# Giving the chain between two scans priority in an interleaved Mamba, FFN and attention kernel

## The chip, the cores and the metric

The kernel runs on one core of one Trainium2 chip. The time is that of the whole program on the device, in microseconds (us), and the figure compared is the median of several runs. Before the change it is 2910.93 us, the median of 3 runs that lie between 2910.67 and 2912.76 us.

A core has five engines, each with a queue of its own that runs in a fixed order: TensorE (PE, matrix products and transposes; its weight loads appear as PEld), VectorE (DVE), ScalarE (ACT), GpSimd (POOL) and SyncE (SP, which here only issues transfers). An instruction waits at the head of its queue until the semaphores it needs are set, and all that stands behind it on that engine waits too.

## The reference, cut to what matters

The input x holds 16 images of 512 positions and 256 channels in float32. Four blocks are added to it in turn:

```python
x = x + mamba(layernorm(x))
x = x + ffn(layernorm(x))
x = x + linear_attention(layernorm(x))
x = x + ffn(layernorm(x))
```

The Mamba block is a recurrence over the 512 positions, with 16 states for each of the 256 channels:

```python
x_in = x @ w_in
dt_low, B, C = split(x_in @ w_x)
dt = softplus(dt_low @ w_dt + b_dt) * 0.099 + 0.001
inp_term[n] = sum_d(dt[d] * A[d, n] * B[n] * x_in[d])      # A = -exp(A_log)
h = exp(dt * A) * h + inp_term
y = h @ C + Dp * x_in
```

The input term has no channel index: it is summed over the channels, so one set of 16 sequences feeds the recurrences of all channels. The feed-forward network (FFN) quantises its input in blocks of 16 to a four-bit grid and back, forms silu(gate) * up with 704 columns, quantises that too, and multiplies by w_down. The attention has 16 heads of 16 channels with the feature map elu + 1 and causal running sums.

## The kernel before, in words

**One image at a time through the scans, the others around it.** The scans of an image are 16 steps in `mamba` (L445). In each, DVE runs one scan instruction over a 128x1024 tile (L485: 128 pairs of channel and state, two such groups one behind the other) and one multiply by C (L489). The tile `bar` of decay factors for it is made by ACT: two exponentials (L466) of a tile `sp` that a transfer has brought (L454: dt, written to DRAM before and read back so that each channel's row lies on 16 partitions), then a square (L469). There are two buffers for `bar` and three for `sp`. PE sums each pair of steps over the states into `py` (L495), which was begun with Dp times u (L483); after eight steps ACT copies `py` to `yT` (L500). Two such copies make y of an image; it is turned by eight transposes into two banks `pt_y` (L508) and DVE adds these to x (L511). x is kept as four chunks of 128 positions.

**What comes before the scans.** `front` (L382) normalises the next image (`layernorm`, L349) and turns it into features (`to_features`, L370); its copies are made while the image before is scanned. `prologue` (L389) then makes, from these features, in this order: z, as `pz` (PE, L396; the product of w_in, w_x and w_dt is folded into one matrix before the loop), with Abs (L405) and Relu (L406) on ACT; u (L412); softplus by Tanh and Ln on ACT (L414, L415) and one multiply-add on DVE (L416), which gives dt; eight transfers of dt to DRAM on SP's queue (L421); C's copy `cm` (L426); dt times u on DVE (L430); its product with A, `pg` (PE, L433); B as `pbm` (PE, L396 again); a copy of it into the tile `inp` (ACT, L439); the multiply of the copy with `pg` (DVE, L440); a copy of that result over the first half of the tile (ACT, L441). The first scan needs `inp`.

The tiles of this chain are shared: `soft`, `dtu` and `yT` are one buffer in turn, and so are `dt` and `inp`; u and cm have one buffer each. z's Abs of the next image therefore can't write before yT of this image has been read by its transposes. PSUM has seven banks in common use (tag "bank": pz, pg, pbm, pt, po and so on, in turn) and one for `py`.

**The FFN.** `ffn` (L517) is called with names that end in `_f` for the first FFN and `_g` for the second: layernorm (bn_stats, the variance plus epsilon at L359, its power -1/2 on POOL at L361 as `rstd`, the normalised chunks at L364 as `xn`), then `fp4` (L208 to L236: on DVE block maxima `amax` at L212, their scales from L217 on, `v` at L226; on ACT `big` at L230; on DVE L232 twice and L234, which writes the quantised values back into the tile), then `tT` (the transposes `pt` at L376, the copies at L377). Then for each of the four chunks and each half of the 704 columns: `pg`, `pu` (PE, L535), Tanh `sg` (ACT, L541), L542 and L545 (DVE); `fp4` again on the chunk's hidden layer; transposes `pt_h` (L561) and copies `hqT` (L565, L570); the product `po` (L574) and its addition to x (L578).

**The interleaving.** All these are Python generators that yield pieces of cost. While image b is scanned, the last FFN of image b-2 runs among its scans; then the first FFN of b and the attention of b-1 take turns, and the pieces of `prologue` for image b+1 are dealt out among the pieces of the first FFN of b (`first`, L781, `weave`, L772, `by_turns`, L811). So the end of the scans of image b, its y, the begin of its first FFN, and the chain from z to the input term of image b+1 stand close together in the program, from the last scan of b to the first scan of b+1: this stretch is called the turn below. Before the loop, `prologue(0)` and `mamba(0)` are woven with the quantisation of the FFN weights (`ffn_weights`, names ending in `_wg`, `_wu`, `_wd`).

**What sets the order.** The framework (Tile) orders the instructions itself before the program runs: among those that are ready in its own model of the machine, it issues the one with the lowest priority number, and an instruction's number is its place in the program text as the generators lay it out. The orders that come out are fixed in each engine's queue.

Of the kernel before, what the change touches and what calls it, by code (L numbers as in the profile page):

```python
# [10 lines left out]
F32 = mybir.dt.float32  # L11
BF16 = mybir.dt.bfloat16
AF = mybir.ActivationFunctionType
ALU = mybir.AluOpType
# [3 lines left out]
P = 128  # L18
# [14 lines left out]
def kernel(  # L33
# [18 lines left out]
    nc = tc.nc  # L52
    B, S, D = x.shape
# [5 lines left out]
    NC = S // P  # L59
    ND = D // P  # L60
# [8 lines left out]
    DT_MIN, DT_MAX = 0.001, 0.1  # L69
# [319 lines left out]
    def prologue(b):  # L389

        xnT = turned.pop(b)

        def from_xn(w, name):
            p = bank(f"{name}_{b}")
            for k in range(ND):
                nc.tensor.matmul(p, w[:, k], xnT[:, k, :], start=(k == 0), stop=(k == ND - 1))  # L396
            return p

        soft = one.tile([P, ND, S], F32, tag="soft", name=f"soft_{b}")
        dt = one.tile([P, ND, S], F32, tag="dt", name=f"dt_{b}")
        for e in range(ND):
            pz = from_xn(w_z_sb[:, :, ts(e, P)], f"pz{e}")
            nc.scalar.activation(soft[:, e, :], pz, AF.Abs, bias=b_dt_sb[:, e : e + 1])  # L405
            nc.scalar.activation(  # L406
                dt[:, e, :], pz, AF.Relu, bias=b_relu[:, e : e + 1], scale=DT_MAX - DT_MIN
            )
        yield 0.5
        u = one.tile([P, ND, S], F32, tag="u", name=f"u_{b}")  # L410
        for e in range(ND):
            nc.scalar.copy(u[:, e, :], from_xn(w_in_sb[:, :, ts(e, P)], f"pu{e}"))  # L412
        yield 0.5
        nc.scalar.activation(soft, soft, AF.Tanh, scale=0.5)  # L414
        nc.scalar.activation(soft, soft, AF.Ln, bias=half_c, scale=0.5 * LN_C)  # L415
        nc.vector.scalar_tensor_tensor(dt, soft, DT_MIN - DT_MAX, dt, ALU.mult, ALU.add)  # L416

        dd = dram.tile([ND, 2, 32, 2, S], F32, tag="dt", name=f"dd_{b}")
        for e in range(ND):
            for q in range(4):  # L420
                nc.sync.dma_start(  # L421
                    dd[e, q // 2, :, q % 2, :], dt[32 * q : 32 * q + 32, e, :]
                )
        yield 1.5
        cm = one.tile([P, S], F32, tag="cm", name=f"cm_{b}")
        nc.scalar.copy(cm, from_xn(w_c_sb, "pcm"))  # L426


        dtu = one.tile([P, ND, S], F32, tag="soft", name=f"dtu_{b}")
        nc.vector.tensor_tensor(dtu, dt, u, ALU.mult)  # L430
        pg = bank(f"pg_{b}")
        for k in range(ND):
            nc.tensor.matmul(  # L433
                pg, a_rep[:, k].rearrange("p n i -> p (n i)"), dtu[:, k, :],
                start=(k == 0), stop=(k == ND - 1),
            )
        pb = from_xn(w_b_sb, "pbm")
        inp = one.tile([P, 2, S], F32, tag="dt", name=f"inp_{b}")
        nc.scalar.copy(inp[:, 0, :], pb)  # L439
        nc.vector.tensor_tensor(inp[:, 1, :], inp[:, 0, :], pg, ALU.mult)  # L440
        nc.scalar.copy(inp[:, 0, :], inp[:, 1, :])  # L441
        begun[b] = (u, dd, inp, cm)
        yield 2.5

    def mamba(b, xt):  # L445
        u, dd, inp, cm = begun.pop(b)

        yT = one.tile([P, ND, S], F32, tag="soft", name=f"yT_{b}")

        def spread(e, j, q0):  # L450

            sp = one.tile([P, 2, S], F32, tag="sp", name=f"sp_{b}_{e}_{j}_{q0}", bufs=NSP)
            src = dd[e, q0 // 2, j * G8 : (j + 1) * G8].rearrange("i q t -> i (q t)")
            nc.sync.dma_start(  # L454
                sp.rearrange("p q t -> p (q t)"),
                src.unsqueeze(0).to_broadcast([NS, G8, 2 * S]),
            )
            return sp

        def decay(sp, e, j, q0):  # L460

            bar = bars[state["bar"] % NBAR]
            state["bar"] += 1
            for i in range(2):
                g = 16 * e + 4 * (q0 + i) + j
                nc.scalar.activation(  # L466
                    bar[:, i, 1:S], sp[:, i, 1:S], AF.Exp, scale=a_col[:, g : g + 1]
                )
            nc.scalar.activation(bar[:, :, 1:S], bar[:, :, 1:S], AF.Square)  # L469
            return bar  # L470

        steps = [(e, j, q0) for e in range(ND) for j in range(4) for q0 in (0, 2)]
        sps = [spread(*steps[at]) for at in range(NSP - 1)]
        ahead = decay(sps[0], *steps[0])
        for at, (e, j, q0) in enumerate(steps):
            bar = ahead
            if at + NSP - 1 < len(steps):
# [7 lines left out]
            nc.vector.tensor_tensor_scan(  # L485
                h.rearrange("p i t -> p (i t)"), bar.rearrange("p i t -> p (i t)"),
                inp.rearrange("p i t -> p (i t)"), 0.0, ALU.mult, ALU.add,
            )
# [12 lines left out]
            yield 3.5  # L501


        for c in range(0, NC, 2):
            pt = bank(f"pt_y_{b}_{c}")
            for i in range(2):
                for e in range(ND):
                    nc.tensor.transpose(  # L508
                        pt[:, ts(i * ND + e, P)], yT[:, e, ts(c + i, P)], ident
                    )  # L510
            nc.vector.tensor_tensor(  # L511
                xt[:, c : c + 2, :], xt[:, c : c + 2, :],
                pt.rearrange("p (c d) -> p c d", d=D), ALU.add,
            )
        yield 1.5

    def ffn(i, nm, xt):  # L517
# [358 lines left out]
```

## Time and profile before

| what | value |
|---|---|
| median of 3 runs | 2910.93 us |
| the profiled execution | 2910.69 us, of which the span of the trace is 2908.9 us |
| mean granted TensorE clock in it | 0.915 |
| scans L485, 256 of them | 578.1 us busy on DVE, 2277 ns each |
| multiplies L489, 256 | 309.2 us busy on DVE, 1213 ns each |
| squares L469, 256, and exponentials L466, 512 | 269.8 and 348.7 us busy on ACT |
| share of the chain that ended last | DVE 55%, PE 29%, ACT 7% |
| POOL busy | 4% |

The span is the time from the first to the last instruction that the profile has; the time of the execution holds 1.8 us more around it. [...] In the view of the groups, each line gives line number, engine, operation, output and inputs by the program's names, busy time in us, and the idle time of the engine just before these instructions with what ended it. In the timeline, a row's first two numbers are start and length in us from the span's start, and square brackets hold the idle time before it and what ended that. In the table of windows, each row is one stretch of time: its bounds and length, then the busy us of PE, PEld, DVE, ACT and POOL in this order (with the number of instructions in parentheses), then the mean granted clock of TensorE, then the transfers' share and rate.

### The profile page before, as it was taken

The numbers are of one execution on the slowest core, as the hardware profiler recorded it, in microseconds if no ns is written. First come the engines' busy times: TensorE is split into PE (matmuls) and PEld (weight loads), VectorE is DVE, ScalarE is ACT, GpSimd is POOL, SyncE is SP. The second block draws the span as 40 slices with busy tenths as digits, with TensorE's granted clock in tenths as the row PEclk, the third lists the DMA queues.
The fourth block names the chain that finished last, engine by engine and source line by source line (L and its number), as shares of the span: only waits on it lengthen the run. The fifth ranks groups of instructions, "written<-read, shape, count | busy, mean of one in ns | idle before, by whom it ended". The sixth has DMA issues, their size and how long they took to land.

```text
span 2908.9 us, 33292 instructions
## 1 busy us (share of the span) xinstructions
PE 2441.2 (84%) x12639; PEld 1428.2 (49%) x12639; DVE 2545.1 (87%) x3795; ACT 1349.0 (46%) x2286; POOL 121.1 (4%) x153
## 2 busy tenths in 40 slices
PE   5676888888888988888888888888888888887887
PEld 2233545454554545455454545545455454545555
DVE  7897889989899898989989898998989999898565
ACT  5555454454545445453545445444544544542122
POOL 2000000000000000000000000000000000000000
PEclk8787899998998999899999999999999899989898
DMA  5332112031321313122031321303122130310000
GB/s 159 87 80 73 51 44 80 15 95 44 80 59 29 81 29 86 53 61 63 21 88 44 80 58 44 80 15 95 44 80 59 36 81 22 84 47 8 1 1 15
DMA packets 64372, 165.21 MB, mean 57 GB/s; under 512 B 8434, under 2 KB 26836, under 8 KB 64212
## 3 DMA queue, kind: packets, MB, share of 16 engines
q1 hardware_dynamic: 62592, 162.03, 21.4%
q8 instruction: 99, 1.62, 0.2%
q10 hardware_dynamic: 1620, 1.06, 0.1%
q14 instruction: 61, 0.50, 0.1%
HBM read 146.28 MB, written 16.78 MB: 56 GB/s over the span
## 4 chain that ended last, share of the span: by engine, by line
DVE 55%; PE 29%; ACT 7%; issue 5%; POOL 2%; POOLq 0%; DVEq 0%; ACTq 0%
DVE h L485 16%; DVE h L489 7%; PE pqk L607 3%; DVE sm L660 2%; PE po_g L574 2%; PE pg_f L535 2%; PE pu_f L535 2%; PE pg_g L535 2%; DVE amax_f L212 2%; PE pu_g L535 2%; PE pz L396 2%; PE py L495 2%; DVE h_f L234 1%; DVE v_f L232 1%; DVE v_f L226 1%
## 5 line engine op out<-in xcount | busy, mean ns | idle before, releaser
L485 DVE TENSOR_TENSOR_SCAN h<-bar,inp 128x1024 f32<-128x1024 f32 x256 | 578.1, 2277 | 10.1 <-ACT inp L441 8.9
L466 ACT ACTIVATE bar<-sp,a_col 128x511 f32<-128x511 f32 x512 | 348.7, 715 | 411.3 <-DVE h L485 410.8
L495 PE MATMUL py<-h,red 128*32 128x512 f32 x1024 | 271.4, 684 | 89.1 <-DVE h L489 89.1
L489 DVE TENSOR_TENSOR h<-h,cm 128x1024 f32<-128x1024 f32 x256 | 309.2, 1213 | 0.0
L469 ACT ACTIVATE bar<-bar 128x1022 f32<-128x1022 f32 x256 | 269.8, 1054 | 4.5
L574 PE MATMUL po_g<-wdT,hqT_g 128*128 128x256 f32 (+1 forms) x768 | 199.8, 403 | 33.1 <-ACT hqT_g L565 33.1
L574 PE MATMUL po_f<-wdT,hqT_f 128*128 128x256 f32 (+1 forms) x768 | 204.7, 410 | 7.8 <-ACT hqT_f L565 7.7
L535 PE MATMUL pg_f<-wgT,tT_f 128*128 128x352 f32 x512 | 200.5, 517 | 2.5 <-DVE sm L660 2.2
L535 PE MATMUL pu_f<-wuT,tT_f 128*128 128x352 f32 x512 | 180.0, 475 | 14.4 <-DVE sm L660 14.4
L574 PEld LDWEIGHTS po_f<-wdT,hqT_f 128*128 128x128 f32 (+1 forms) x768 | 141.4, 197 | 96.3 <-issue 26.8
L574 PEld LDWEIGHTS po_g<-wdT,hqT_g 128*128 128x128 f32 (+1 forms) x768 | 138.3, 193 | 94.3 <-ACT hqT_g L565 47.2
L535 PE MATMUL pg_g<-wgT,tT_g 128*128 128x352 f32 x512 | 178.4, 471 | 0.0
L535 PE MATMUL pu_g<-wuT,tT_g 128*128 128x352 f32 x512 | 173.5, 461 | 0.0
L660 DVE TENSOR_TENSOR sm<-psc,causal 128x512 f32<-128x512 f32 x256 | 163.5, 680 | 9.9 <-PE psc L653 7.9
L230 ACT ACTIVATE big_f<-v_f 128x704 bf16<-128x704 f32 (+1 forms) x80 | 67.3, 841 | 203.2 <-DVE v_f L226 203.0
L535 PEld LDWEIGHTS pu_f<-wuT,tT_f 128*128 128x128 f32 x512 | 100.9, 199 | 79.1 <-DVE sm L660 21.7
L607 PE MATMUL pqk<-tT_a,w_qkv_sb 128*128 128x512 f32 x256 | 135.6, 670 | 0.7 <-ACT tT_a L377 0.7
L535 PEld LDWEIGHTS pg_g<-wgT,tT_g 128*128 128x128 f32 x512 | 97.8, 195 | 74.9 <-issue 37.1
L535 PEld LDWEIGHTS pg_f<-wgT,tT_f 128*128 128x128 f32 x512 | 94.7, 205 | 70.5 <-issue 17.7
L535 PEld LDWEIGHTS pu_g<-wuT,tT_g 128*128 128x128 f32 x512 | 98.1, 192 | 55.1 <-issue 1.5
L495 PEld LDWEIGHTS py<-h,red 128*32 128x32 f32 x1024 | 36.4, 114 | 176.8 <-DVE h L489 118.0
L541 ACT ACTIVATE sg_g<-pg_g 128x352 f32<-128x352 f32 x128 | 58.8, 459 | 108.2 <-PE pg_g L535 108.0
(224 smaller groups left out, 4483.8 us busy)
## 6 DMA issues: line engine op xcount, KB each, us to landing
sp<-dd SPq DMA_DIRECT2D x256, 512.0 KB, 4.6
x<-in_L_attn_a_x_dram SPq DMA_DIRECT2D x16, 512.0 KB, 4.7
dd<-dt SPq DMA_DIRECT2D x128, 64.0 KB, 1.7
out_dram<-x SPq DMA_DIRECT2D x16, 512.0 KB, 3.0
w_qkv_sb<-in_L_attn_b_W_attn_dram ACTq DMA_DIRECT2D x1, 768.0 KB, 6.8
raw_d<-in_L_ffn_w_down_dram SPq DMA_DIRECT2D x1, 704.0 KB
raw_g<-in_L_ffn_w_gate_dram SPq DMA_DIRECT2D x1, 640.0 KB, 6.4
raw_u<-in_L_ffn_w_up_dram SPq DMA_DIRECT2D x1, 640.0 KB, 6.2
```

What stands on the lines that cost most here:

```text
L212: nc.vector.tensor_reduce(amax, src.rearrange("p (b k) -> p b k", k=BLK), AX.X, ALU.max, apply_absolute_value=True,)
L230: nc.scalar.activation(big, v, AF.Abs, scale=STEP)
L466: nc.scalar.activation(bar[:, i, 1:S], sp[:, i, 1:S], AF.Exp, scale=a_col[:, g : g + 1])
L469: nc.scalar.activation(bar[:, :, 1:S], bar[:, :, 1:S], AF.Square)
L485: nc.vector.tensor_tensor_scan(h.rearrange("p i t -> p (i t)"), bar.rearrange("p i t -> p (i t)"), inp.rearrange("p i t -> p (i t)"), 0.0, ...
L489: nc.vector.tensor_tensor(h, h, cm.unsqueeze(1).to_broadcast([P, 2, S]), ALU.mult)
L495: nc.tensor.matmul(py[32 * q : 32 * q + 32, :], red[:, j, :], (h0, h)[q // 2][:, q % 2, :], start=False, stop=(j == 3),)
L535: nc.tensor.matmul(pw[:, :HF], xqT[:, k, ts(c, P)], wT[:, k, cols], start=(k == 0), stop=(k == ND - 1),)
L541: nc.scalar.activation(sg, pg[:, :HF], AF.Tanh, scale=0.5)
L574: nc.tensor.matmul(po[:, :D], hqT[:rows, r, :], wdT[:rows, r, :], start=(r == 0), stop=(r == NR - 1),)
L607: nc.tensor.matmul(pz, w_qkv_sb[:, k, ts(je, P)], xnT[:, k, :], start=(k == 0), stop=(k == ND - 1),)
L660: nc.vector.tensor_tensor(t, psc[g].rearrange("p (s t) -> p s t", t=P), causal.unsqueeze(1).to_broadcast([P, NH // 4, P]), ALU.mult,)
```

## The change

Five blocks of the program text are wrapped in `with tc.high_priority():`. Instructions that are issued inside it get the priority numbers of the program's begin instead of that of their place, so that in the framework's ordering they go ahead of all other instructions that are ready at the same time. What they wait for stays the same. The blocks are, in `prologue`: z with its Abs and Relu; u; Tanh, Ln, dt and the transfers of dt; C's copy, dt times u, `pg`, `pbm` and the three instructions on `inp`. In `mamba`: the copy `yT`, and the turning of y with its addition to x. The rest of the program, the sizes, the buffers and the number of instructions are as before. The lines move: what is L485 before is L489 after, L489 is L493, L416 is L419, L440 is L444, L535 is L541.

```diff
@@ -396,50 +396,54 @@
                 nc.tensor.matmul(p, w[:, k], xnT[:, k, :], start=(k == 0), stop=(k == ND - 1))
             return p
 
-        soft = one.tile([P, ND, S], F32, tag="soft", name=f"soft_{b}")
-        dt = one.tile([P, ND, S], F32, tag="dt", name=f"dt_{b}")
-        for e in range(ND):
-            pz = from_xn(w_z_sb[:, :, ts(e, P)], f"pz{e}")
-            nc.scalar.activation(soft[:, e, :], pz, AF.Abs, bias=b_dt_sb[:, e : e + 1])
-            nc.scalar.activation(
-                dt[:, e, :], pz, AF.Relu, bias=b_relu[:, e : e + 1], scale=DT_MAX - DT_MIN
-            )
+        with tc.high_priority():
+            soft = one.tile([P, ND, S], F32, tag="soft", name=f"soft_{b}")
+            dt = one.tile([P, ND, S], F32, tag="dt", name=f"dt_{b}")
+            for e in range(ND):
+                pz = from_xn(w_z_sb[:, :, ts(e, P)], f"pz{e}")
+                nc.scalar.activation(soft[:, e, :], pz, AF.Abs, bias=b_dt_sb[:, e : e + 1])
+                nc.scalar.activation(
+                    dt[:, e, :], pz, AF.Relu, bias=b_relu[:, e : e + 1], scale=DT_MAX - DT_MIN
+                )
         yield 0.5
-        u = one.tile([P, ND, S], F32, tag="u", name=f"u_{b}")
-        for e in range(ND):
-            nc.scalar.copy(u[:, e, :], from_xn(w_in_sb[:, :, ts(e, P)], f"pu{e}"))
+        with tc.high_priority():
+            u = one.tile([P, ND, S], F32, tag="u", name=f"u_{b}")
+            for e in range(ND):
+                nc.scalar.copy(u[:, e, :], from_xn(w_in_sb[:, :, ts(e, P)], f"pu{e}"))
         yield 0.5
-        nc.scalar.activation(soft, soft, AF.Tanh, scale=0.5)
-        nc.scalar.activation(soft, soft, AF.Ln, bias=half_c, scale=0.5 * LN_C)
-        nc.vector.scalar_tensor_tensor(dt, soft, DT_MIN - DT_MAX, dt, ALU.mult, ALU.add)
-        dd = dram.tile([ND, 2, 32, 2, S], F32, tag="dt", name=f"dd_{b}")
-        for e in range(ND):
-            for q in range(4):
-                nc.sync.dma_start(
-                    dd[e, q // 2, :, q % 2, :], dt[32 * q : 32 * q + 32, e, :]
-                )
+        with tc.high_priority():
+            nc.scalar.activation(soft, soft, AF.Tanh, scale=0.5)
+            nc.scalar.activation(soft, soft, AF.Ln, bias=half_c, scale=0.5 * LN_C)
+            nc.vector.scalar_tensor_tensor(dt, soft, DT_MIN - DT_MAX, dt, ALU.mult, ALU.add)
+            dd = dram.tile([ND, 2, 32, 2, S], F32, tag="dt", name=f"dd_{b}")
+            for e in range(ND):
+                for q in range(4):
+                    nc.sync.dma_start(
+                        dd[e, q // 2, :, q % 2, :], dt[32 * q : 32 * q + 32, e, :]
+                    )
         yield 1.5
-        cm = one.tile([P, S], F32, tag="cm", name=f"cm_{b}")
-        nc.scalar.copy(cm, from_xn(w_c_sb, "pcm"))
-        dtu = one.tile([P, ND, S], F32, tag="soft", name=f"dtu_{b}")
-        nc.vector.tensor_tensor(dtu, dt, u, ALU.mult)
-        pg = bank(f"pg_{b}")
-        for k in range(ND):
-            nc.tensor.matmul(
-                pg, a_rep[:, k].rearrange("p n i -> p (n i)"), dtu[:, k, :],
-                start=(k == 0), stop=(k == ND - 1),
-            )
-        pb = from_xn(w_b_sb, "pbm")
-        inp = one.tile([P, 2, S], F32, tag="dt", name=f"inp_{b}")
-        nc.scalar.copy(inp[:, 0, :], pb)
-        nc.vector.tensor_tensor(inp[:, 1, :], inp[:, 0, :], pg, ALU.mult)
-        nc.scalar.copy(inp[:, 0, :], inp[:, 1, :])
-        begun[b] = (u, dd, inp, cm)
+        with tc.high_priority():
+            cm = one.tile([P, S], F32, tag="cm", name=f"cm_{b}")
+            nc.scalar.copy(cm, from_xn(w_c_sb, "pcm"))
+            dtu = one.tile([P, ND, S], F32, tag="soft", name=f"dtu_{b}")
+            nc.vector.tensor_tensor(dtu, dt, u, ALU.mult)
+            pg = bank(f"pg_{b}")
+            for k in range(ND):
+                nc.tensor.matmul(
+                    pg, a_rep[:, k].rearrange("p n i -> p (n i)"), dtu[:, k, :],
+                    start=(k == 0), stop=(k == ND - 1),
+                )
+            pb = from_xn(w_b_sb, "pbm")
+            inp = one.tile([P, 2, S], F32, tag="dt", name=f"inp_{b}")
+            nc.scalar.copy(inp[:, 0, :], pb)
+            nc.vector.tensor_tensor(inp[:, 1, :], inp[:, 0, :], pg, ALU.mult)
+            nc.scalar.copy(inp[:, 0, :], inp[:, 1, :])
+            begun[b] = (u, dd, inp, cm)
         yield 2.5
 
     def mamba(b, xt):
@@ -497,21 +501,23 @@
                         start=False, stop=(j == 3),
                     )
             if j == 3 and q0 == 2:
-                nc.scalar.copy(yT[:, e, :], py)
+                with tc.high_priority():
+                    nc.scalar.copy(yT[:, e, :], py)
             yield 3.5
 
 
-        for c in range(0, NC, 2):
-            pt = bank(f"pt_y_{b}_{c}")
-            for i in range(2):
-                for e in range(ND):
-                    nc.tensor.transpose(
-                        pt[:, ts(i * ND + e, P)], yT[:, e, ts(c + i, P)], ident
-                    )
-            nc.vector.tensor_tensor(
-                xt[:, c : c + 2, :], xt[:, c : c + 2, :],
-                pt.rearrange("p (c d) -> p c d", d=D), ALU.add,
-            )
+        with tc.high_priority():
+            for c in range(0, NC, 2):
+                pt = bank(f"pt_y_{b}_{c}")
+                for i in range(2):
+                    for e in range(ND):
+                        nc.tensor.transpose(
+                            pt[:, ts(i * ND + e, P)], yT[:, e, ts(c + i, P)], ident
+                        )
+                nc.vector.tensor_tensor(
+                    xt[:, c : c + 2, :], xt[:, c : c + 2, :],
+                    pt.rearrange("p (c d) -> p c d", d=D), ALU.add,
+                )
         yield 1.5
 
     def ffn(i, nm, xt):
```

More of the change, by code (lines that the diff above doesn't have):

```diff
@@ L416, in prologue @@
-        nc.vector.scalar_tensor_tensor(dt, soft, DT_MIN - DT_MAX, dt, ALU.mult, ALU.add)
-        dd = dram.tile([ND, 2, 32, 2, S], F32, tag="dt", name=f"dd_{b}")
-        for e in range(ND):
-            for q in range(4):
-                nc.sync.dma_start(
-                    dd[e, q // 2, :, q % 2, :], dt[32 * q : 32 * q + 32, e, :]
-                )
-        yield 1.5
-        cm = one.tile([P, S], F32, tag="cm", name=f"cm_{b}")
-        nc.scalar.copy(cm, from_xn(w_c_sb, "pcm"))
-        dtu = one.tile([P, ND, S], F32, tag="soft", name=f"dtu_{b}")
@@ new lines, in prologue @@
+        yield 1.5
+        with tc.high_priority():
[8 more added lines that the diff above has]
+                    start=(k == 0), stop=(k == ND - 1),
+                )
+            pb = from_xn(w_b_sb, "pbm")
[4 more added lines that the diff above has]
+            begun[b] = (u, dd, inp, cm)
```

## The prediction

> **What bounds the kernel now.** I read the page's first two parts, then the waits of DVE (VectorE), then one turn between two images in the timeline, engine by engine, and last the clock in that turn.
>
> ```profile
> PE 2441.2 (84%) x12639; PEld 1428.2 (49%) x12639; DVE 2545.1 (87%) x3795; ACT 1349.0 (46%) x2286; POOL 121.1 (4%) x153
> DVE  7897889989899898989989898998989999898565
> ```
>
> DVE is the engine that sets the time: 87% over the span, 8 or 9 tenths in every slice from the eighth to the 37th. What can be won is its idle time only, since the change removes no instruction. From image 3 on the first scans of two images lie 171.8 and 172.9 us apart in turn (436.6, 608.4, 781.3, 953.1 us in the timeline), of which DVE idles about 16. The waits say where:
>
> ```profile
> DVE inp L440 <- ACT inp L439: 56.0, 11, 5.5
> DVE inp L440 <- DMA sp<-dd: 19.6, 4, 4.9
> DVE xn_f L364 <- POOL rstd_f L361: 3.0, 3, 1.1
> ```
>
> The first two are the same wait, of L440 for the input term, put down to one releaser or the other: 75.6 us in 15 turns, 5 us in each, right before the first scan of an image. Followed back in the turn to image 8 (rows of DVE, PE and ACT, columns start and length in us):
>
> ```profile
> 1264.59 0.68 DVE L511 TENSOR_TENSOR x<-x,pt_y 128x512 f32<-128x512 f32 x1
> 1270.13 0.17 DVE L359 TENSOR_SCALAR var_f<-mv_f 128x4 f32<-128x4 f32 x1
> 1277.37 1.22 DVE L416 SCALAR_TENSOR_TENSOR dt<-soft,dt 128x1024 f32<-128x1024 f32 x1
> 1284.17 1.22 DVE L234 TENSOR_TENSOR xn_f<-v_f,half_f 128x1024 f32<-128x1024 f32 x1
> 1296.49 0.69 DVE L440 TENSOR_TENSOR inp<-inp,pg 128x512 f32<-128x512 f32 x1 [4.90 <-ACT inp L439]
> 1297.86 4.47 DVE L485 TENSOR_TENSOR_SCAN h<-bar,inp 128x1024 f32<-128x1024 f32 x2 [0.68 <-ACT inp L441]
> ...
> 1285.45 1.84 PE L376 MATMUL pt_f<-ident,xn_f 128*128 128x128 f32 x8 [4.06 <-DVE xn_f L234]
> 1287.11 2.39 PE L535 MATMUL pg_f<-wgT,tT_f 128*128 128x352 f32 x4
> 1289.34 1.35 PE L535 MATMUL pu_f<-wuT,tT_f 128*128 128x352 f32 x4
> 1293.95 1.88 PE L396 MATMUL pbm<-tT_m,w_b_sb 128*128 128x512 f32 x4
> ...
> 1295.87 0.59 ACT L439 COPY inp<-pbm 128x512 f32<-128x512 f32 x1 [1.89 <-PE pbm L396]
> 1297.21 0.62 ACT L441 COPY inp<-inp 128x512 f32<-128x512 f32 x1
> ```
>
> So the scan waits for the input term, that for pbm, and pbm stands in PE's queue behind pt_f and the feed-forward's pg_f and pu_f, which wait for xn_f of image 7 (4.06 us of idle PE). What ends the turn is thus xn_f, which is not in the prioritised blocks, and PE's order behind it. dt, which the change also hastens, ends at 1278.6 and is not last: its first spread tile was issued at 1282.4 and landed 4.7 later, at 1287.1, and both bars were done at 1294.0.
>
> ```profile
> 1275.00:1280.00 5.00, 5.00 (x14) 2.28 (x12) 4.63 (x9) 4.96 (x6) 0.00 (x0) 1.00 0.07 17
> 1285.00:1290.00 5.00, 4.55 (x15) 3.10 (x16) 3.77 (x6) 3.44 (x7) 0.00 (x0) 0.66 1.04 250
> 1113.00:1118.00 5.00, 5.00 (x14) 3.10 (x13) 3.68 (x5) 4.01 (x7) 0.00 (x0) 0.50 0.88 193
> ```
>
> The granted clock (the number after POOL's) is full before PE's idle 4 us and 0.66 after them; in the turn before (third row) it stays at 0.50 throughout, and that turn is 1.2 us longer (44.1 against 42.9 from last scan to first).
>
> **The change, part by part.** The instructions and their number are unchanged; only places in the queues differ. SP's and POOL's orders are the same in both programs, the eight dd writes and the spread loads included. For DVE, PE and ACT the order differs in the same places in each of the 13 turns to images 3 to 15, in the filling up to image 2, and at the tail in two weight passes of one product.
>
> *y's turn.* Two transposes of pt_y (0.44 for two in their row) now precede py's last passes, so yT comes 0.44 later; pt_y is then done at 1263.75, and DVE is in L234 of h_g until 1263.79: worth 0 by 0.04, and 0.4 a turn if that cover is gone. L511 then passes amax and L217: 0.8 earlier for x, inside the next sum.
>
> *xn_f (DVE), from 1263.79 in the turn shown.* Start to start, 20.38 us pass to L234. L212 and L217 of amax_g now follow it: -0.80 - 0.09. Two waits for sg (0.53 and 0.23) with the overlap they broke, some 1.0 together, go, because sg now stands later in DVE's order than its ACT. New: L364 directly follows var; the row has 1.28 us from var to L364, covered there by L578 and L234, so 1.2 are now bare. And v_f's L232 waits 0.3 for big_f, which ACT can begin only when v_f ends. Sum -0.89 - 1.0 + 1.2 + 0.3 = -0.4, with two lost overlaps less certain; bounds -1.0 (those waits nearly covered) and +0.8 (big_g_2 late: it now stands behind the first soft and dt, ready by my sum at 1269.6, needed at 1270.4).
>
> *dt.* pz passes five of six matmuls of po_g and both soft/dt pairs pass big_g; Ln no longer waits for sg. DVE's L416 starts at about 1275.2 by the same walk, 2.1 earlier, and on SP the eight dd writes and the spread loads behind them start and land 2.1 earlier. u's products pass one matmul of pu_g, and u is needed at L430 only, at about 1281. The 4.9 us wait hides all this: worth 0 alone. If dt were the last, it would be worth up to 2.1.
>
> *PE behind xn_f.* The second matmul of pu_f is passed by pcm, pg and pbm: 1.18 start to start for both, so -0.59. ACT's first exp for bar now stands between the two tT_f copies (0.66, its data now there by 1285) where big_g stood (0.70, and it waited for v_g): -0.2, bounds -0.4 and +0.7 (spread tile late).
>
> *L441.* The first hqT copy still stands between L439 and L441. pt_h is behind the passed matmul, so that copy starts about 0.5 after L439 and ends later than L440: +0.35, bounds 0 and +0.6.
>
> *After the first scan.* The next hqT copies stand behind an exp that waits for the second scan: po_g and the next pg_f, pu_f slip by some 1.5 us against the scans. DVE's L545 four steps on had 0.1 us of slack by my walk, so +0.25; bounds 0 and +0.6. After that PE catches up, since it waits for DVE's sm there.
>
> *The clock.* With PE's idle stretch about 0.5 shorter, fewer turns should be of the longer kind (0.50 throughout). Bounds: -1.2 (all as good as no dip at all, from the difference of the two kinds) and +0.6 (all of the longer kind, half of 1.2). I take -0.3, nearer to no effect.
> [...]
>
> Per turn: -0.4 - 0.6 - 0.2 + 0.35 + 0.25 - 0.3 = -0.9, times 13 = -12 us.
>
> *Filling.* ACT now issues u, cm, u and big_wu before image 0's second soft. big_wu needs v_wu (ends 33.95), 1.4 long, then soft, dt, Tanh, load and Ln, 0.59 + 0.57 + 1.06 + 1.28 + 1.15: Ln at 40.0 instead of 35.0. DVE comes to L416 after v_wd at 41 instead of 35.5. The first scan moves from 50.5 to about 55.7; DVE fills 5.2 us with statistics that stood between the scans, and bare scan-multiply pairs then take 3.4 instead of 3.65 us each, so that 1.6 remain lost. In the turn to image 2, attention 0's four L364 (0.33 each) and var leave a stretch where DVE then waited 1.02 anyway and stand among the scans with a bare 1.1 us wait for rstd: +2.6. In the turns to images 1 and 2, L441 stands behind an sg whose product lies behind the passed pu_f: no gain. Together +4, bounds 0 and +7. Tail: 0 (two passes change place), bounds -3 and +3 for the clock's phase.
>
> **Sum.** The profiled execution took 2910.69 (span 2908.9 and 1.8 around it), 0.24 under the median of 2910.93. 2910.7 - 12 + 4 = 2903; the uncertain xn_f term leans to the gain (the two lost overlaps), so 2902.
>
> **Rivals.**
> 1. *The clock dip goes.* Turns lose another 1.2 us each: -2.0 x 13 + 4 gives 2889. For: both kinds of turn alternate in lockstep with full and half clock, so a small shift may break it. Against: shorter PE waits (2.6 us before L713) also have 0.5 stretches behind them.
> 2. *Nothing that counts moves.* xn_f stays where it is and only the passed matmul counts: (-0.6 + 0.35) x 13 = -3, plus 4: 2912, no change. For: the last wait hangs on xn_f, outside the blocks.
> 3. *Slower: the bare rstd wait.* If DVE's stretch to xn_f gets longer by 1 us (1.2 for rstd and big_g late on top, the sg waits not gone), xn_f moves to +1.0 and the turn to +1.0 - 0.8 + 0.35 + 0.25 = +0.8: +10 + 4 gives 2925. It decides from xn_f about 0.3 us later than before on: then the turn gains nothing and the filling's loss stands. For: ACT's queue now holds soft and dt ahead of big_g. Against: 0.8 us of slack in my walk.
>
> **Chances.** Forecast (2896 to 2905) 0.42, rival 1 0.18, rival 2 0.22, rival 3 0.18. About 0.2%, 5.8 us, is what a measurement of this kernel can tell from no change: faster 0.60, same 0.22, slower 0.18. The range for 8 in 10 runs from 2887, near rival 1, to 2918, into rival 3.
>
> **What would show it.** In the changed profile: L234 of xn_f some 28.1 us after the start of the last L489 (1255.70 to 1284.17, 28.5, now); a DVE wait of about 1 us for rstd_f in each of 13 turns (three in all now); L440's wait still the largest, about 4 us; 0.5 to 1.5 us less from last scan to first; the first scan at 55 to 56 us. Wrong I would be if the turn is not set by pbm, if the scans' 128.9 us from first to last change by over 0.5, or if the clock's halved stretches move off the turns.

## The result, and the profile after

The changed kernel takes 2940.49 us (median of 4 runs, 2940.27 to 2942.10) against 2911.04 us of the kernel before (4 runs, 2910.67 to 2912.76): a ratio of 1.0101 with a 95% interval of 1.0084 to 1.0119. It is 29.5 us slower, where 2902 was forecast. The profiled execution's span grew by 29.7 us, from 2908.9 to 2938.6.

The page's first part and the waits of DVE in the changed kernel (waited for: us in total, times, longest):

```profile
PE 2446.2 (83%) x12639; PEld 1448.0 (49%) x12639; DVE 2547.6 (87%) x3795; ACT 1350.3 (46%) x2286; POOL 122.5 (4%) x153
```

```profile
DVE inp L444 <- ACT inp L443: 44.5, 13, 4.4
DVE sg_f L548 <- ACT sg_f L547: 39.0, 21, 2.7
DVE x L584 <- PE po_g L580: 27.7, 17, 6.2
DVE h_f L551 <- PE pu_f L541: 19.9, 18, 5.8
DVE xn_f L364 <- POOL rstd_f L361: 17.6, 16, 1.1
```

DVE is busy for nearly the same time (2547.6 against 2545.1 us, in a span that is 29.7 us longer), so 27 of these 29.7 us are time in which it is idle. The wait for the input term fell as forecast, from 56.0 + 19.6 us to 44.5 + 4.4 (the smaller part, put down to the spread loads, stands further down that list). The wait for rstd_f rose from 3.0 to 17.6, as forecast too. What is new stands between them: sg_f (8.2 before), po_g (16.1) and pu_f (7.0) together make 86.6 us instead of 31.3. In the steady turns they stand behind the first scans of an image, not in the turn.

The same place in the timeline, the turn to image 9 and what follows (start and length in us):

```profile
1457.89 0.41 DVE L364 TENSOR_SCALAR xn_f<-x,mv_f,rstd_f 128x256 f32<-128x256 f32 x1 [1.12 <-POOL rstd_f L361]
1471.44 1.22 DVE L234 TENSOR_TENSOR xn_f<-v_f,half_f 128x1024 f32<-128x1024 f32 x1
1482.92 0.69 DVE L444 TENSOR_TENSOR inp<-inp,pg 128x512 f32<-128x512 f32 x1 [3.61 <-ACT inp L443]
1484.47 4.47 DVE L489 TENSOR_TENSOR_SCAN h<-bar,inp 128x1024 f32<-128x1024 f32 x2 [0.42 <-ACT inp L445]
1496.04 0.42 DVE L584 TENSOR_TENSOR x<-x,po_g 128x256 f32<-128x256 f32 x1 [1.02 <-PE po_g L580]
1499.18 0.52 DVE L548 SCALAR_TENSOR_TENSOR sg_f<-sg_f,pg_f 128x352 f32<-128x352 f32 x1 [2.72 <-ACT sg_f L547]
1500.40 0.52 DVE L551 SCALAR_TENSOR_TENSOR h_f<-sg_f,pu_f 128x352 f32<-128x352 f32 x1 [0.69 <-PE pu_f L541]
...
1486.95 0.88 PE L567 MATMUL pt_h_g<-ident,h_g 128*128 128x128 f32 x6
1490.22 5.79 PE L580 MATMUL po_g<-wdT,hqT_g 128*128 128x256 f32 x12 [2.39 <-ACT hqT_g L571]
1495.93 2.71 PE L541 MATMUL pg_f<-wgT,tT_f 128*128 128x352 f32 x4
...
1486.79 1.33 ACT L470 ACTIVATE bar<-sp,a_col 128x511 f32<-128x511 f32 x2 [2.04 <-DVE h L489]
1488.97 0.72 ACT L470 ACTIVATE bar<-sp,a_col 128x511 f32<-128x511 f32 x1 [0.85 <-DVE h L489]
1489.60 0.73 ACT L571 COPY hqT_g<-pt_h_g 128x512 f32<-128x512 f32 x2
```

Read it backwards. DVE waits 1.02 + 2.72 + 0.69 = 4.43 us for po_g, sg_f and pu_f. PE has them late because po_g began only at 1490.22, after 2.39 us of idle time, and then took 5.79 us. It waited for the copies hqT, and these stand on ACT behind an exponential (1488.97) that waits for the second scan. Before, this exponential stood behind the copies: po_g waited 1.19 and took 3.05.

The kernel before, at the same place of the turn to image 8, which the prediction shows:

```profile
1302.04 3.05 PE L574 MATMUL po_g<-wdT,hqT_g 128*128 128x256 f32 x12 [1.19 <-ACT hqT_g L565]
1305.02 1.45 PE L535 MATMUL pg_f<-wgT,tT_f 128*128 128x352 f32 x4
```

The windows there, after and before (the granted clock is the number behind POOL's):

```profile
1486.00:1490.00 4.00, 1.83 (x10) 0.90 (x8) 4.00 (x4) 2.36 (x4) 0.00 (x0) 0.92 0.13 22
1490.00:1494.00 4.00, 3.78 (x9) 3.07 (x10) 3.97 (x4) 3.31 (x7) 0.00 (x0) 0.50 0.52 127
1494.00:1498.00 4.00, 4.00 (x9) 1.95 (x8) 1.45 (x2) 1.14 (x2) 0.00 (x0) 0.50 0.55 161
```

```profile
1303.00:1307.00 4.00, 4.00 (x16) 2.59 (x15) 4.00 (x3) 2.54 (x4) 0.00 (x0) 1.00 0.75 223
```

Behind PE's 2.39 us of idle time the clock is 0.50; before, behind 1.19 us, it stays at 1.00 through po_g and pg_f.

Where the 29.7 us lie, by the starts of first scans and the ends of last scans in the timelines (us; period and turn are means over the ten stretches between the first scans of images 4 and 14, the scans over images 4 to 14):

| | first scan of image 0 | of 3 | of 15 | period | last scan to first | first scan to last | image 15's first scan to the end |
|---|---|---|---|---|---|---|---|
| before | 50.5 | 436.6 | 2505.1 | 172.37 | 43.47 | 128.90 | 403.9 |
| after | 56.7 | 442.5 | 2529.0 | 174.08 | 41.70 | 132.39 | 409.6 |

The filling loses 5.9 us up to image 3, the twelve periods to image 15 lose 18.0, and the end 5.7. The turn is 1.8 us shorter, and the scans behind it are 3.5 us longer.

### The profile page after: what moved, and what is told of

Same layout as the page of the kernel before. It is cut to its first block, busy times and chain, and to the rows that moved or that the text cites. A ratio compares the mean times of both kernels' runs of the same rounds, so it can differ in the third digit from the quotient of the medians.

```text
span 2938.6 us, 33281 instructions
## 1 busy us (share of the span) xinstructions
PE 2446.2 (83%) x12639; PEld 1448.0 (49%) x12639; DVE 2547.6 (87%) x3795; ACT 1350.3 (46%) x2286; POOL 122.5 (4%) x153
## 4 chain that ended last, share of the span: by engine, by line
DVE 58%; PE 28%; issue 6%; ACT 4%; POOL 3%; DMA 0%; SPq 0%; POOLq 0%; DVEq 0%; ACTq 0%
DVE h L489 15%; DVE h L493 5%; PE po_g L580 3%; PE pg_f L541 3%; PE pqk L613 3%; DVE sm L666 3%; PE pu_f L541 3%; DVE amax_f L212 2%; PE pg_g L541 2%; DVE v_f L226 2%; PE pu_g L541 2%; DVE v_f L232 2%; DVE v_g L233 2%; DVE h_f L234 2%; DVE v_f L233 1%
## 5 line engine op out<-in xcount | busy, mean ns | idle before, releaser
L489 DVE TENSOR_TENSOR_SCAN h<-bar,inp 128x1024 f32<-128x1024 f32 x256 | 578.0, 2276 | 10.6 <-ACT inp L445 5.5
L499 PE MATMUL py<-h,red 128*32 128x512 f32 x1024 | 261.5, 671 | 95.9 <-DVE h L493 95.9
L493 DVE TENSOR_TENSOR h<-h,cm 128x1024 f32<-128x1024 f32 x256 | 309.2, 1213 | 0.9
L580 PE MATMUL po_g<-wdT,hqT_g 128*128 128x256 f32 (+1 forms) x768 | 235.8, 454 | 48.2 <-ACT hqT_g L571 48.2
L580 PEld LDWEIGHTS po_g<-wdT,hqT_g 128*128 128x128 f32 (+1 forms) x768 | 158.1, 220 | 125.0 <-ACT hqT_g L571 62.2
L541 PE MATMUL pg_f<-wgT,tT_f 128*128 128x352 f32 x512 | 206.2, 530 | 0.5 <-ACT tT_f L377 0.5
L541 PE MATMUL pu_f<-wuT,tT_f 128*128 128x352 f32 x512 | 183.6, 477 | 18.5 <-DVE sm L666 18.5
L541 PE MATMUL pg_g<-wgT,tT_g 128*128 128x352 f32 x512 | 181.2, 477 | 0.0
L541 PE MATMUL pu_g<-wuT,tT_g 128*128 128x352 f32 x512 | 178.4, 462 | 0.0
L541 PEld LDWEIGHTS pu_f<-wuT,tT_f 128*128 128x128 f32 x512 | 101.9, 201 | 88.5 <-DVE sm L666 25.8
L541 PEld LDWEIGHTS pg_f<-wgT,tT_f 128*128 128x128 f32 x512 | 99.4, 211 | 68.5 <-issue 24.9
L541 PEld LDWEIGHTS pg_g<-wgT,tT_g 128*128 128x128 f32 x512 | 96.6, 195 | 71.3 <-issue 29.2
L541 PEld LDWEIGHTS pu_g<-wuT,tT_g 128*128 128x128 f32 x512 | 97.5, 193 | 56.1 <-issue 8.7
L547 ACT ACTIVATE sg_f<-pg_f 128x352 f32<-128x352 f32 x128 | 58.2, 455 | 110.4 <-PE pg_f L541 110.4
```

What stands on the lines that cost most here:

```text
L489: nc.vector.tensor_tensor_scan(h.rearrange("p i t -> p (i t)"), bar.rearrange("p i t -> p (i t)"), inp.rearrange("p i t -> p (i t)"), 0.0, ...
L499: nc.tensor.matmul(py[32 * q : 32 * q + 32, :], red[:, j, :], (h0, h)[q // 2][:, q % 2, :], start=False, stop=(j == 3),)
L541: nc.tensor.matmul(pw[:, :HF], xqT[:, k, ts(c, P)], wT[:, k, cols], start=(k == 0), stop=(k == ND - 1),)
L580: nc.tensor.matmul(po[:, :D], hqT[:rows, r, :], wdT[:rows, r, :], start=(r == 0), stop=(r == NR - 1),)
```

## The experiments

All were compared with the kernel before on the same chip. Diffs are against the changed kernel unless said otherwise.

### e1: PE's new wait filled

```diff
             po = bank(f"po_{nm}_{c}")
+            if nm[0] == 'g' and c == 3:
+                for i in range(8):
+                    nc.tensor.transpose(po[:, D : D + P], h[:, ts(i % 4, P)], ident)
```

> The changed kernel, with 8 transposes more between the last pt_h and the last po_g of the second feed-forward, into the unused half of that po's bank; no other place in any queue differs. They fall into the 2.39 us in which PE waits for hqT after the scans have begun (8 of about 0.2 us each, so some 0.8 us of idle are left). Theory A (the loss is the halved clock that follows this wait: po_g 5.79 instead of 3.05, pg_f 2.71 instead of 1.45): the dip of 10.2 us at +4.9 us goes, third to fourth scan falls from 28.6 to 24.0 to 24.5, the period from 174.1 to about 170, 2885 to 2905 us in all. Theory B (the loss is the later place of the hqT copies itself, the clock only follows): unchanged within 5 us, 2935 to 2945. Theory C (the clock falls there for the idle 3.9 us before pt_f): the dip stays, 2935 to 2945, with the clock at half through po_g.

Measured: 2908.19 us, ratio 0.9987 (0.9978 to 0.9996), so the loss is gone. The timeline and one window, at the same place:

```profile
1475.53 1.04 PE L580 MATMUL po_g<-ident,h_g 128*128 128x128 f32 x8
1478.08 3.05 PE L583 MATMUL po_g<-wdT,hqT_g 128*128 128x256 f32 x12 [1.52 <-ACT hqT_g L571]
1481.06 1.45 PE L541 MATMUL pg_f<-wgT,tT_f 128*128 128x352 f32 x4
```

```profile
1478.00:1482.00 4.00, 3.92 (x15) 2.79 (x16) 3.97 (x4) 3.31 (x7) 0.00 (x0) 1.00 0.61 162
```

The copies hqT come no earlier than in the changed kernel; po_g still starts 5.8 us after the first scan. Only the idle time before it is 1.52 instead of 2.39 us, and the clock is full there. Third to fourth scan falls from 28.6 to 24.5 us (23.9 before), first to last from 132.39 to 129.47. So of the 3.5 us, the halved clock at this place costs at least 2.9 and the later place of hqT at most 0.6: e1 has another stretch of halved clock about 15 us after the first scan, and in two of eleven images, where it lasts 6.8 us instead of 3.4, the scans take 131.2. Theory A holds for the mechanism. The total is 3 us over its range: the mean period is 171.3 us where about 170 was expected, and filling and end are still late (first scan of image 3 at 444.8, 408.4 from image 15 to the end).

### e2 and e3: all but the last block, and the last block alone

In e2 the block of C's copy, dt times u, pg, pbm and inp has no priority; in e3 it alone has.

```diff
-        with tc.high_priority():
+        with nullcontext():
             cm = one.tile([P, S], F32, tag="cm", name=f"cm_{b}")
```

> Priority on y's turn, z, u and dt, none on the last block (C's copy, dt times u, pg, pbm, input term). xn_f comes as in the changed kernel, while ACT's queue after the input term is that of before (both hqT pairs ahead of the exponentials that wait for the second scan). Theory A (the last block alone makes the loss, by moving an exponential ahead of hqT): first to last scan is 128.9 again, the turn about 1 us shorter than before, 2900 to 2912 us. Rival (the loss comes from xn_f with the bare wait for rstd, or from ACT's big_g behind soft and dt): 2930 to 2945.

> Priority on the last block alone (C's copy, dt times u, pg, pbm, input term). xn_f, y, z and dt stand as before; ACT has three exponentials ahead of the second hqT pair as in the changed kernel. Theory A: third to fourth scan is 26 to 29 us instead of 23.9, with PE idle about 2.4 us before po_g and a halved clock behind it; the turn only 0.3 to 0.6 us shorter; 2930 to 2955 us. Rival (the loss needs the earlier xn_f or z): within 5 us of before.

Measured: e2 2899.29 us, ratio 0.9958 (0.9944 to 0.9972); e3 2940.40, ratio 1.0097 (1.0084 to 1.0111). In e2 the scans take 128.60 us and the turn 42.07, and the period is 170.67. In e3 the row of po_g has the changed kernel's 2.39 us of idle time in every turn. In the turn to image 9 what follows is the same too:

```profile
1491.82 5.79 PE L580 MATMUL po_g<-wdT,hqT_g 128*128 128x256 f32 x12 [2.39 <-ACT hqT_g L571]
1497.53 2.71 PE L541 MATMUL pg_f<-wgT,tT_f 128*128 128x352 f32 x4
```

In ten of the twelve turns to images 3 to 14 of e3 the clock is halved there for 3.4 us instead of 10.2, and in five of these for 6.8 us more some 17 us after the first scan; the scans take 131.7 us on average. The last block by itself makes the loss in the turns; the other four make the gain, and more of it without the last one. e2's total is 0.7 us under its range, e3's within it.

### e4: the copies ahead of the exponential

In `down`, the transposes pt_h and the copies hqT of the second feed-forward's last chunk get priority as well.

```diff
-            hqT = act.tile([P, NR, P], F32, tag="hqT", name=f"hqT_{nm}_{c}", bufs=2)
-            for r0 in range(0, NR, 4):
...
+            with tc.high_priority() if nm[0] == 'g' and c == 3 else nullcontext():
+                hqT = act.tile([P, NR, P], F32, tag="hqT", name=f"hqT_{nm}_{c}", bufs=2)
+                for r0 in range(0, NR, 4):
...
```

> The changed kernel, with the transposes pt_h and the copies hqT of the last chunk of the second feed-forward given priority too: ACT then has both hqT pairs right after the input term and the three exponentials behind them; on PE the five last passes of one po_g follow the other pt_h. Theory A (the place of hqT behind the exponential is the cause, through PE's idle time): PE's wait before the last po_g falls under 1.2 us, third to fourth scan to about 24, the turn stays at 41.6 to 42; period about 170.5 and 2885 to 2900 us. Theory C (the clock falls for PE's 3.9 us before pt_f): the clock is halved at +5 us all the same and the time stays at 2930 or more.

Measured: 2901.27 us, ratio 0.9961 (0.9948 to 0.9973), 1 us over its range. PE's rows at the place:

```profile
1469.45 0.82 PE L568 MATMUL pt_h_g<-ident,h_g 128*128 128x128 f32 x6
1470.10 5.50 PE L581 MATMUL po_g<-wdT,hqT_g 128*128 128x256 f32 x22
1475.53 1.45 PE L541 MATMUL pg_f<-wgT,tT_f 128*128 128x352 f32 x4
```

22 instructions, five of the six products of one po_g and all six of the next (two instructions each), run without a wait in less time than 12 took. With five blocks in priority and the copies ahead of the exponential again, the turn keeps its gain (41.70) and the scans take 129.03 us. e1 takes away the halved clock and leaves the order, e4 takes away the order: each recovers over 30 us. The chain of causes is thus shown at both links: order on ACT, PE idle for 2.39 us, clock halved.

### e5 and e10: the filling

e5 is e2 with priority only from image 2 on; e10 is the kernel before with priority on u alone, for images 0 and 1 alone.

```diff
-        with tc.high_priority():
+        with tc.high_priority() if b > 1 else nullcontext():
```

> As the run without priority for the input term (y, z, u and dt only), and these only from image 2 on, so that the filling (images 0 and 1) keeps the order of before. Theory: the filling loses because u's products and copies delay image 0's second soft; then the first scans of images 0 and 1 are at 50.5 and 140.9 us again instead of 55.7 and 146.4, the turns stay at a period of 170.7, and the total is 4 to 7 us under the 2899.3 of that run, 2892 to 2895. Rival (the later first scans only reorder DVE's work and cost nothing in the end): 2898 to 2901.

> Priority on u's product and copy alone, and only for images 0 and 1; all the rest as before. If u makes the filling's loss (its copies and big_wu ahead of image 0's second soft): first scan of image 0 at 54 to 57 us instead of 50.5, image 2's 5 to 9 us later than 253.5, 2915 to 2922 us. Rival (the loss is that of several blocks together): 2910 to 2914.

Measured: e5 2890.71 us, ratio 0.9929 (0.9916 to 0.9941), 8.6 us under e2 and 1.3 under the range of its theory; its first scans of images 0, 1 and 2 are at 50.7, 141.3 and 253.4 us, and image 3's at 434.1 instead of 442.0. e10 takes 2917.91, ratio 1.0021 (1.0012 to 1.0029): first scan at 55.2, image 3's at 443.9, and the same period as before. u's block alone makes the filling's loss. ACT's rows show how, the kernel before first and the changed one below:

```profile
30.36 0.68 ACT L406 ACTIVATE dt<-pz,b_relu 128x512 f32<-128x512 f32 x1
33.84 1.15 ACT L415 ACTIVATE soft<-soft,half_c 128x1024 f32<-128x1024 f32 x1
```

```profile
30.05 0.57 ACT L414 COPY u<-pu 128x512 f32<-128x512 f32 x1
34.24 1.48 ACT L230 ACTIVATE big_wu<-v_wu 128x1536 bf16<-128x1536 f32 x1 [2.65 <-DVE v_wu L226]
35.63 0.67 ACT L406 ACTIVATE soft<-pz,b_dt_sb 128x512 f32<-128x512 f32 x1
39.19 1.15 ACT L418 ACTIVATE soft<-soft,half_c 128x1024 f32<-128x1024 f32 x1
```

u is copied where z's second half was worked on, which now stands behind big_wu and its wait for DVE; Ln comes 5.35 us later, and the first scan 6.2.

### e6 and e7: y's turn alone, z alone

> Priority on y's turn alone (yT's copy, its transposes, the addition to x). On DVE x is finished before amax of the other feed-forward, the waits for sg stay, one pass of 0.8 us stays between var and xn_f so that some 0.4 us of rstd are bare. If each block adds its own part: xn_f 0.3 to 0.6 us earlier, 2903 to 2910 us. If the steps of the clock decide (periods seen so far are 172.35 on average, 174.08 and 170.67 us), either 2910 to 2913 or 2888 to 2894. Rival (y without z gains nothing, since xn_f waits for the same work): 2909 to 2913.

> Priority on z alone (pz, Abs, Relu). DVE's xn_f passes are then mixed with v and dt as in the changed kernel, the two waits for sg are gone, the wait for rstd is bare (about 1.1 us in each turn), amax still precedes. If the walk of the prediction holds (-1.0 for sg, +1.2 for rstd): xn_f within 0.3 us of before, 2906 to 2915 us. Rival (z is what brings the gain of the run without the input term's priority): 2892 to 2903.

Measured: e6 2912.05 us, ratio 0.9999 (0.9990 to 1.0008); e7 2932.85, ratio 1.0070 (1.0058 to 1.0083). L234 of xn_f starts 29.29 and 29.30 us after the last scan's end (29.16 before, 28.28 in e2), with a bare wait for rstd of 0.90 and 1.12. Alone, neither gains; together with u and dt they give e2's 0.9 us at xn_f. In e7 the turn even grows to 45.09 us, which was outside all that was expected. Its rows behind xn_f:

```profile
1122.54 2.71 PE L541 MATMUL pg_f<-wgT,tT_f 128*128 128x352 f32 x4 [0.64 <-ACT tT_f L377]
...
1119.45 1.33 ACT L470 ACTIVATE bar<-sp,a_col 128x511 f32<-128x511 f32 x2 [4.31 <-DMA sp<-dd]
1121.22 0.79 ACT L230 ACTIVATE big_g<-v_g 128x704 bf16<-128x704 f32 x1 [0.44 <-DVE v_g L226]
1121.92 1.05 ACT L377 COPY tT_f<-pt_f 128x512 f32<-128x512 f32 x2
```

It is e3's fault in another place: on ACT, instructions that wait for a transfer and for DVE now stand ahead of the copies tT_f that PE waits for, and pg_f follows late and at half clock (2.71 us): it starts 2.56 us after pt_f, where it was 1.66 and 1.79 in the two kinds of turn before, and the stretch of halved clock there is 6.8 us long in every turn, where it was so in every second one before. This is read from the rows; no run tried e7 with these copies first. The gains of the blocks don't add: each changes the order that the scheduler finds for the others. Priority on u alone or dt alone in the turns was not tried.

### e8: the chain made longer

e2, with pbm's first pass made three times:

```diff
             p = bank(f"{name}_{b}")
+            for k in [0] * (2 if name == "pbm" else 0):
+                nc.tensor.matmul(p, w[:, k], xnT[:, k, :], start=True, stop=True)
```

> As the run without priority for the input term, with two passes of pbm's product made twice, each 0.43 us by pbm's row, in every turn on the path to the input term; all orders else are the same. If time adds up along the chain: 0.86 us in each of 15 turns, 2910 to 2913 us against 2899.3. If the period keeps to multiples of the clock's step (all turns of that run are 170.67 us, of the changed kernel 174.08, half the sum of two turns of before 172.35; their differences are 1.7 us, half of the 3.4 us in which the granted clock changes): the period stays at 170.67 with a shifted dip and the total within 3 us of 2899, or goes to 172.4 and the total to 2919 to 2924.

Measured: 2928.24 us, ratio 1.0054 (1.0042 to 1.0067), 29 us over e2. Neither expectation holds as it stands, and both put the addition too small: a product of pbm is two instructions of 0.43 us, so two more products are 1.72 us a turn and not 0.86. PE's rows show them (L396 the added ones, L398 those of before):

```profile
1130.85 1.88 PE L396 MATMUL pbm<-tT_m,w_b_sb 128*128 128x512 f32 x4
1132.57 1.88 PE L398 MATMUL pbm<-tT_m,w_b_sb 128*128 128x512 f32 x4
```

By this size, time that adds up along the chain would give 2899.3 + 15 x 1.72 = 2925, 3 us under the measured time. From last scan to first, the turn grows by 1.8 us (42.07 to 43.85). The periods go in a cycle of three, 171.70 + 173.54 + 173.59 = 518.83 us, on which the last section has more.

### e9 and e11: PE's old wait filled too

e5, with transposes before those of pt_f, 16 in e9 and 28 in e11:

```diff
             pt = bank(f"pt_{name}_{k}")
+            if k == 0 and name[0] == "f":
+                for i in range(16):
+                    nc.tensor.transpose(pt[:, ts(i % NC, P)], ident, ident)
```

> As the run with y, z, u and dt from image 2 on, with 16 transposes more into the bank of pt_f, before its own, in the 3.6 us in which PE waits for xn_f in each turn (some 0.16 us each, so about 1 us of idle is left); the other engines' orders are the same. If the halved clock behind pt_f comes from this idle time: the dip of 3.4 us at -11.8 us goes, pg_f and pu_f take 1.45 and 1.35 us instead of 2.71 and 1.50, the turn is up to 1.4 us shorter: 2868 to 2876 us if that adds up or the period goes from 170.67 to 168.96, 2889 to 2892 if the period holds at 170.67. Rival (the clock falls there whatever PE does, or the transposes delay pt_f): no dip less, 2890 or more.

> As the run with 16 transposes in the wait for xn_f, with 28 (about 0.11 us each by that run, so some 0.5 us of idle are left instead of 1.8). If the idle stretch before pt_f makes the dip, it is now gone in every turn, not in every second one, and xn_f to first scan is 11.2 us in all turns instead of 11.2 and 12.9 in alternation. If these 0.85 us a turn add up: 2875 to 2878 us. If the mean period holds to whole steps of 1.7 us: 2886 to 2889 with the dips elsewhere (170.67 us, as in the two runs before), or 2862 to 2867 (168.96). Rival (28 transposes overrun and delay pt_f): 2890 or more.

Measured: e9 2886.86 us, ratio 0.9915 (0.9902 to 0.9929); e11 2870.19, ratio 0.9854 (0.9839 to 0.9870). In e9, 1.8 us of idle are left, and the dip behind pt_f is gone in every second turn: xn_f to first scan takes 11.20 and 12.89 us by turns (12.58 in all turns of e5). But the scans behind a shorter turn take longer, 129.4 us instead of 128.8, and the mean period stays at 170.7: there the clock is halved for 3.4 us from 13.7 us after the first scan on. Two windows show it for image 4, whose first scan is at 603.04:

```profile
613.20:616.60 3.40, 3.40 (x50) 2.94 (x49) 3.16 (x7) 2.12 (x4) 0.00 (x0) 1.00 0.77 204
616.70:620.00 3.30, 3.30 (x9) 2.30 (x9) 2.44 (x4) 0.88 (x2) 0.00 (x0) 0.50 0.93 252
```

By the profile PE is busy without a break before this fall (3.40 of 3.40 us), with many narrow products of the attention, the last of them 16 of 128x8. So idle time is not the only thing that comes before a halved clock here; what makes this one was not tried. For the total, the gain over e5 is mostly that of the end, 403.7 instead of 406.6, and 2886.86 is 2 us under the range for a period that holds. In e11 xn_f to first scan takes 11.20 us in every turn:

```profile
1092.95 3.22 PE L377 MATMUL pt_f<-ident 128*128 128x128 f32 x28
1096.01 1.02 PE L490 MATMUL py<-u,d_diag 128*128 128x512 f32 x2
1097.55 1.09 PE L379 MATMUL pt_f<-ident,xn_f 128*128 128x128 f32 x8 [0.53 <-DVE xn_f L234]
1098.89 1.45 PE L544 MATMUL pg_f<-wgT,tT_f 128*128 128x352 f32 x4 [0.24 <-ACT tT_f L380]
```

pg_f takes 1.45 us instead of 2.71 in e2's turns, and the mean period is 169.3. e11's total lies in none of the three ranges put for it, 5 us under the one for time that adds up and 3 over the one for a shorter period. e11 beats both kernels, 42 us under before (2912.69 in that comparison) and 70 under the changed one, with work added to PE.

### e12: the best parts together

All five blocks from image 2 on, with the edits of e4 and e11.

> All five blocks of the change from image 2 on, the last pt_h and hqT given priority too, and the 28 transposes in the wait for xn_f. The sum of what the runs before showed: the input term's block with hqT ahead (turn 0.4 us shorter than without that block), the filling as before, no dip before the chain. If it adds up: 2868 to 2876 us; if the period holds at 170.67: 2885 to 2892. Rival (the input term's block costs time even with hqT ahead): slower than the run with 28 transposes and without it by 3 us or more.

Measured: 2887.76 us, ratio 0.9915 (0.9902 to 0.9928), 17.6 us over e11. The number fits two of the forecasts, the rival and the period that holds (170.75 us on average). Turn 40.61 (40.69 in e11), but scans 130.13 us (128.63). That the last block alone costs this is not shown: e4 has the same block and copies and 129.03. In e12 the clock is halved for 3.4 us some 14 us after the first scan of every image from 3 to 14, in e11 after three of five, in e4 at no such place from image 4 on. Against e4 the turn is 1.1 us shorter and the scans 1.1 longer. So it looks like e9's case, and how much is the block's was not separated.

## Why the prediction was wrong

The forecast was faster, and the kernel is slower. Step by step:

- **y's turn, 0.** Held: alone it changes nothing (e6).
- **xn_f, -0.4.** Held. From the start of the last L493 to that of L234 of xn_f it was to take 28.1 us and takes 27.93 (28.47 before); the bare wait for rstd is 1.12 in each turn, as put.
- **dt, worth 0.** Not tried alone. With all blocks the last wait is still for inp, 3.61 us in the rows shown.
- **PE behind xn_f, L441 and the clock in the turn.** With xn_f these steps gave -0.4 - 0.6 - 0.2 + 0.35 - 0.3 = -1.15 for last scan to first; measured 43.47 to 41.70, -1.8. The sign was right; e4 keeps the whole of it, e2 has 42.07.
- **After the first scan, +0.25, bounds 0 and +0.6.** This is the step that failed: measured +3.5. It had named the place, the cause (hqT behind an exponential that waits for the second scan) and the slip, "some 1.5 us"; po_g starts 5.75 us after the first scan instead of 4.18, a slip of 1.57. It priced the slip as if PE ran on at full speed. e1 shows that the slip alone stays within these bounds (at most 0.6); the 2.9 us more go with the halved clock, which is there behind 2.39 us of idle PE and is not behind 1.19 (before) or 1.52 (e1). The prediction had named the sign that it would be wrong: scans that change by over 0.5 us, or halved stretches that move off the turns. Both came.
- **The clock, -0.3, bounds -1.2 and +0.6.** Wrong by its scope: it looked for the halved clock only where it was before, in front of the turn, and not at the wait that another step of the same sum made longer. The row that should have warned stands under the prediction's first rival: PE waits of 2.6 us that "also have 0.5 stretches behind them" (in the kernel before, the wait of 2.56 us that ends at 1344.29 is followed by a clock of 0.50 up to 1350.4).
- **The filling, +4, bounds 0 and +7.** +5.9 up to image 3, within the bounds, but not by the sum given. The first scan is at 56.7 where 55.7 was put, by the mechanism given, and e10 shows that u is the cause. But of its delay only 1.6 us were to be left after image 0's scans, and image 1's first scan is still 5.9 late (146.8 instead of 140.9); image 2's is 8.4 late (261.9 instead of 253.5), and the turn to image 3 and the scans before it give 2.5 back. That the sum came near is luck.
- **The tail, 0, bounds -3 and +3.** +5.7 from image 15's first scan on, of which 3.3 are its scans (131.4 instead of 128.1), which have the same fault, and 2.5 what follows the last one (278.2 instead of 275.7).

The third rival forecast a slower kernel, but from xn_f being late through the bare wait for rstd. That wait came and xn_f is earlier all the same, so it was not this rival that won. Its price, 2925, was also too small. The first rival's -2.0 a turn is -2.1 by its own terms (-0.9 - 1.2), which changes nothing here.

## What to carry to other kernels

When a step of a sum makes an engine wait longer, ask what the engine does after the wait, not only when it starts: here po_g took 3.05 us behind 1.19 us of idle PE and 5.79 us, with the clock at 0.50, behind 2.39. Priority on a chain changes the order around it too; look in the queues of the other engines for an instruction that now waits in front of one that was free, and try the blocks one by one, since one of them may hold the whole loss. Where PE must wait in a turn, try spare transposes that keep it busy: 28 of them took e11 20.5 us under e5 (2870.19 against 2890.71). But compare whole periods: in e9 and e12 the time came back behind the first scans.

## What the runs showed of the hardware

In the steady turns of before and after the trace has the granted clock at 0.50 for stretches of 3.413, 6.827, 10.240 or 13.653 us, all multiples of the first, and at 1.00 between them. After a few turns most of the kernels repeat a cycle that comes out as a whole number of the same length (174.08 / 51 = 3.4133 us):

| kernel | cycle, us | turns in it | lengths of 3.4133 us |
|---|---|---|---|
| before | 344.7 | 2 | 101 |
| after | 174.08 | 1 | 51 |
| e2, e5 | 170.67 | 1 | 50 |
| e7 | 174.07 | 1 | 51 |
| e8 | 518.8 | 3 | 152 |
| e9 | 341.3 | 2 | 100 |
| e11 | 846.5 | 5 | 248 |

In these kernels savings and losses in the chain didn't reach the period one to one: 1.72 us more in e8 became 2.3 us a turn (170.67 to 172.94), and in e9 every second turn lost its dip and the mean period didn't move. Behind e9's shorter turns, and behind e12's, which are shorter than e4's, the clock was halved for 3.4 us some 14 us after the first scan. Of the kernels not in the table, e4 settles at e2's cycle, e6 and e10 at that of before, e3 at 102 lengths in two turns and e1 at 251 in five; e12 settles at none within its turns. What sets the length of 3.413 us, and why a dip comes back at that place in e9, no run here shows.
